# Layer 1's paired panels with feature sums as the stationary operand, and two of the last pair's four tiles scored by TensorE

## The chip, the cores and the metric

The kernel runs on one core of one Trainium2 chip. A run's time is the device time of that core in microseconds, from the start of the launch to its end. The profile is of one such execution: its span goes from the first to the last instruction, and every start time in a profile row counts from the start of that span. The engines are TensorE (PE for matrix products, PEld for loading their stationary operand), VectorE (DVE), ScalarE (ACT), GpSimd (POOL, which also issues the gathers and scatters) and SyncE (SP, which issues most transfers).

## The reference

Two layers of the same form work on 3327 tokens of 256 features, padded here to 3328 = 26 tiles of 128. Each layer first mixes tokens with the sparse matrix `adj` and then sends every token to two of eight experts.

```
x = x + relu(adj @ (ln(x) @ W) + b)                       # layer 0, mixing
x = x + sum over the 2 best of 8 experts (relu MLP, 1024 hidden) of ln(x)
A = tanh(adj*adj) where adj > 0, at most 700 entries a row # layer 1, mixing
x = x + relu(A @ (tanh(ln(x) @ Wp + bp) @ Wg) + bg)
x = x + ln(x) + sum over the 2 best of 8 experts (gelu MLP, 256 hidden) of ln(x)
```

`ln` is a layer norm without gain or offset. The two best experts come from a product with a 256 x 8 matrix, the router (plus a bias in layer 0). All arithmetic that matters here is float32.

## The kernel before

**Panels and pieces.** The output tokens of a mixing step are cut into 13 panels of 256 tokens. The transposed matrix of a panel comes in two pieces, each of 13 chunks of 128 source tokens by 256 output tokens (1664 KB). Six buffers called `ring` hold pieces; a piece that is used up gives its buffer to the next load. Layer 1 turns each piece into tanh(max(a, 0)^2) in place, by passes on DVE (line 653, where the maximum is taken) and ACT (line 660).

**Pairs by seven products.** Panels are handled two at a time where possible: layer 0 takes panels 0 and 1 singly, then (2,3) to (10,11) as pairs, then 12 singly; layer 1 takes 0 singly, (1,2) to (9,10) as pairs, then 11 and 12 singly. A pair's 2 x 2 block product (two panels, two halves of the feature columns) is done with seven block products instead of eight, from sums of pieces (`add_pieces`, line 459, in place) and sums of feature halves (`half_sums`, made once a layer and held in `pad`). Each block product is 13 chunks deep. The features themselves lie in `s`, tokens on partitions.

**Two orientations.** In layer 0 `product` (line 449) makes the feature half the stationary operand and streams 256 piece columns, so the result has features on partitions; it is copied to SBUF and multiplied by the weight matrix later (`weigh`, line 485), which brings tokens back onto partitions. In layer 1 `multiply` (line 679) makes a 128 x 128 block of the piece the stationary operand and streams 128 feature columns, twice for each chunk, so the result already has tokens on partitions. In the profile a float32 matmul has two records, so a block product is 26 records of 256 columns in layer 0 and 52 records of 128 columns in layer 1.

**What follows a pair in layer 1.** ACT copies partial results from PSUM to `h2T` tiles (line 664), DVE adds others (lines 716, 735, 740), then `add_sums` adds the bias (line 691) and takes max(., 0) plus `x` (line 692). The panels' routing (`route1`) is a dictionary of small steps that the next unit calls by name through `step`, from hooks placed between its own matmuls: statistics (DVE), normalized tiles `xn` (ACT, line 361), turned tiles `pt` (TensorE, line 388), scores `pg` by TensorE (line 826) or by DVE (line 818), the choice of two (`rt_both`, line 854), the positions `pr` (TensorE, lines 923 and 924) and at last the scatter of tokens into the experts' lists (POOL, line 945). In `single`, the hooks are counted in matmuls from 0 to 51.

**The join of layer 0's mixing and its experts.** While panel 12 of layer 0 is multiplied (line 474), `finish` weighs the panels (10, 11) and calls `route0` for their four tiles: layer norm, then eight DVE instructions for each tile (line 818) that multiply and sum `xn` with one row of the router, then the choice. The positions (line 923) of these tiles stand in TensorE's order after the first expert block's 32 hidden-layer records (line 1378) and the weighing of panel 12 (line 485).

**Order.** Each engine runs its instructions in the order in which a scheduler put them; the scheduler orders by estimated cost and data dependence, and `behind(...)` pins an instruction after another. An engine whose next instruction waits holds up everything behind it on that engine. The experts' blocks of layer 1 begin to load while panels 11 and 12 are still being multiplied; `place_of` (line 1397) is DVE's conversion of the loaded token numbers of a block into scatter indices.

Of the kernel before, what the change touches and what calls it, by code (L numbers as in the profile page):

```python
# [128 lines left out]
def gnn_moe_two_layers(  # L129
# [198 lines left out]
    last_normalized, last_shift, last_turned, last_pass = [], [], [], []  # L328
# [72 lines left out]
    def add_relu(x_tile, ps, b_sb):  # L401

        t = work.tile([P, D], F32, name="gnn_t", bufs=2)
        nc.vector.tensor_tensor(t, ps, b_sb, ALU.add)
        nc.vector.scalar_tensor_tensor(x_tile, t, 0.0, x_tile, ALU.max, ALU.add)
# [55 lines left out]
    def aggregate_first(b_sb, w, w_sb, begin, count, route, listed, freed):  # L461
# [29 lines left out]
        def finish():  # L491
            if not waiting:
                return
            todo = list(waiting)
            waiting.clear()
            if todo[0][0] < NPAN - 1:
                listed()
            for pan, g in todo:
                for it in range(PW // P):
                    weigh(pan, g, it)  # L500
            if todo[0][0] == NPAN - 1:
                listed()
            for _ in route([pan for pan, _ in todo]):
                pass
# [123 lines left out]
        rest(NPAN - 1, 0, {CJ: layer0.turn_first}, LAST_BEHIND)  # L628
        return finish

    def aggregate(b_sb, route, freed, turn, copied):
# [31 lines left out]
        def copy(out, ps):  # L663
            copied.append(nc.scalar.copy(out, by_tile(ps)))

        def sums_of():

            g = work.tile([P, 2, D], F32, name="h2T", bufs=2)
            return g, [g[:, :, ts(h, P)] for h in range(DC)]

        def by_tile(ps):
            return ps.rearrange("p (i d) -> p i d", d=P)

        def multiply(ps, a, b, first=True, hooks=()):
            hooks = dict(hooks)
            ps = by_tile(ps)
            for c in range(CJ):
                for it in range(PW // P):
                    nc.tensor.matmul(  # L679
                        ps[:, it, :], lhsT=a[:, c, ts(it, P)], rhs=b[:, c, :],  # L680
                        start=(first and c == 0 and it == 0), stop=(c == CJ - 1),
                        skip_group_check=True,
                    )
                if c in hooks:
                    hooks[c]()

        b_tiles = b_sb.unsqueeze(1).to_broadcast([P, 2, D])

        def add_sums(pan, g):
            x_t = x[:, pan * 2 : pan * 2 + 2, :]  # L690
            nc.vector.tensor_tensor(g, g, b_tiles, ALU.add)
            nc.vector.scalar_tensor_tensor(x_t, g, 0.0, x_t, ALU.max, ALU.add)

        def pair(p1, p2, step, ps_x, ps_q, ps_b, ps_z):
# [4 lines left out]
            multiply(ps_x, a11, b11)  # L699
            (g1, (c11, c12)), (g2, (c21, c22)) = sums_of(), sums_of()  # L700
            copy(c11, ps_x)
# [6 lines left out]
            multiply(ps_q, a22, t4)  # L708
            copy(c21, ps_q)
# [5 lines left out]
            multiply(ps_b, a12, b21)  # L715
            nc.vector.tensor_tensor(c11, c11, by_tile(ps_b), ALU.add)
# [3 lines left out]
            multiply(ps_z, a21, t1, hooks={2: turn_, 7: turn_})  # L720
            run(1)
            copy(c22, ps_z)
            free(p2, 0)
            score = lambda: step("scores")
            multiply(ps_x, a22, t2, False, {2: score, 6: score})
            step("weights")
            copy(c12, ps_x)
# [5 lines left out]
            multiply(ps_z, a12, b22, False)  # L733
            free(p1, 1)
            nc.vector.tensor_tensor(c12, c12, by_tile(ps_z), ALU.add)
            add_sums(p1, g1)
            multiply(ps_x, a11, t3, False, {2: lambda: step("listed"), 8: lambda: step("planned")})
            filter_next(True)
            for part in (c21, c22):
                nc.vector.scalar_tensor_tensor(  # L740
                    part, part, -1.0, by_tile(ps_x), ALU.mult, ALU.subtract
                )
            add_sums(p2, g2)
# [37 lines left out]
        for u in UNITS[1]:  # L781
# [3 lines left out]
            else:  # L785
                hooks = {
                    0: lambda: step("statistics", "normalized"),
                    2: lambda: step("other scores"),
                    16: lambda: step("turned"),
                    18: lambda: step("turned"),  # L790
                    28: lambda: step("scores"),
                    30: lambda: step("scores", "weights", "exponentials"),
                    42: lambda: step("listed"),
                    48: lambda: step("planned"),
# [14 lines left out]
    def scores(xns, n, all_n=None):  # L809
        sc = work.tile([P, all_n or n, E], F32, name="rt_sc", bufs=2)  # L810
        for g in range(n):
            score_tile(xns[g // 2][:, g % 2, 0, 0:D], sc[:, g, :])
        return sc
# [401 lines left out]
    def experts(xlist, ys, group, fixed, n_hidden, func, w1T, b1, w2T, b2, copy, order_of_places, kept=None,  # L1215
# [176 lines left out]
        def place_of(t, late):  # L1392
            xb, col, n = loaded[t][1], col_of(t), groups_of(t)
            index = work.tile([P, SG], I32, name="index", bufs=6)[:, 0:n]
            with behind(last_y):
# [235 lines left out]
    f1_r_sb = const.tile([P, DC, E], F32, name="f1_r_sb")  # L1631
    f1_b1_sb = const.tile(list(f1_b1.shape), F32, name="f1_b1_sb")
    g1_bp_sb = const.tile(list(g1_bp.shape), F32, name="g1_bp_sb")
    for t, w in [
        (gnn_b_sb, g0_b[0:1, :].partition_broadcast(P)),
        (g1_wg_sb, g1_wg.rearrange("(c p) n -> p c n", p=P)),
        (f1_r_sb, f1_rT.rearrange("(c p) n -> p c n", p=P)),
        (f1_b1_sb, f1_b1),
# [21 lines left out]
    def route0(pans):  # L1660
# [5 lines left out]
        sc = scores(xns, n)  # L1666
# [30 lines left out]
    by_feature(None, g1_wp, proj_sb)  # L1697
    nc.gpsimd.dma_start(out=gnn_b_sb, in_=g1_bg[0:1, :].partition_broadcast(P))
# [491 lines left out]
```

## Time and profile before

| | us |
|---|---|
| median of three runs (1183.0, 1186.75, 1187.92) | 1186.75 |
| the profiled execution, whole time | 1181.27 |
| its span | 1179.5 |
| TensorE busy (97% of the span) | 1138.9 |
| VectorE busy (72%) | 851.9 |
| ScalarE busy (51%) | 603.9 |
| GpSimd busy (27%) | 318.5 |

The mean granted TensorE clock over the span is 0.991 of full speed. The span falls into layer 0's mixing (to about 309 us), its experts (to about 692 us), the features of layer 1 (to about 744 us), layer 1's panel 0 (to 767 us), its five pairs (767 to 981 us), panels 11 and 12 (981 to 1037 us), its experts (to about 1161 us) and the last outputs. A matmul's duration in a row is longer than its distance to the next one, since matmuls overlap; costs on TensorE are therefore read from the distance between the starts of neighbouring groups in the timeline, not from durations. A row of the timeline gives start, length, engine, line, operation, result and inputs, shape, count, and in brackets the idle time before it and what ended that idle time.

### The profile page before, as it was taken

How to read it: one execution, taken by the hardware profiler on the slowest of the kernel's cores; microseconds unless marked ns; L12 is line 12 of the kernel's file. 1: busy time of each engine (PE TensorE's matmuls, PEld its weight loads, DVE VectorE, ACT ScalarE, POOL GpSimd, SP SyncE). 2: the span in 40 equal slices, each digit the busy share in tenths (PEclk: the TensorE clock that was granted, in tenths of full speed). 3: DMA queues.
4: the chain of work that ended last, by engine and by line, in shares of the span. 5: the costliest groups of instructions: out<-in, count | busy, mean ns of one | idle time of the engine just before them, and what ended most of it. 6: DMA issues, size and time to landing. Idle time of an engine off the chain costs nothing. (4 is left out here: it accounts for less than half of the span.)

```text
span 1179.5 us, 21265 instructions
## 1 busy us (share of the span) xinstructions
PE 1138.9 (97%) x7093; PEld 1018.9 (86%) x7093; DVE 851.9 (72%) x2667; ACT 603.9 (51%) x1110; POOL 318.5 (27%) x367
## 2 busy tenths in 40 slices
PE   8999999999899999999999999999999997999983
PEld 7888888888788888888898888899999997888862
DVE  6799999988975555454545669486898896886464
ACT  5599657450323333434333336988769774043331
POOL 2211232242331112111111010022245244365442
PEclk9999999999999999999999999999999998999997
DMA  9895737724376555857665956125536633377696
GB/s 348 187 316 217 258 118 234 259 91 151 130 258 231 193 188 185 276 183 242 209 206 182 376 209 229 61 104 206 186 141 211 218 136 130 96 250 236 222 298 229
DMA packets 123190, 241.78 MB, mean 205 GB/s; under 512 B 24480, under 2 KB 93120, under 8 KB 116160
## 3 DMA queue, kind: packets, MB, share of 16 engines
q1 hardware_dynamic: 108656, 205.59, 52.3%
q0 software_dynamic: 11136, 31.60, 7.2%
q10 hardware_dynamic: 3280, 3.15, 0.8%
q8 instruction: 58, 0.95, 0.3%
q14 instruction: 60, 0.49, 0.1%
HBM read 203.98 MB, written 36.33 MB: 204 GB/s over the span
## 5 line engine op out<-in xcount | busy, mean ns | idle before, releaser
L1386 ACT ACTIVATE pad<-ps_h,ring 128x256 f32<-128x256 f32 (+1 forms) x282 | 128.6, 457 | 281.4 <-PE ps_h L1378 153.5
L1378 PE MATMUL ps_h<-pad,ring 128*128 128x256 f32 (+1 forms) x1184 | 253.4, 366 | 3.5 <-ACT pad L1328 3.2
L1378 PEld LDWEIGHTS ps_h<-pad,ring 128*128 128x128 f32 x1184 | 200.2, 190 | 46.1 <-ACT pad L1386 10.0
L945 POOL DMA_INDIRECT ys<-pad,index x114 | 115.8, 1016 | 360.3 <-DVE pad L1433 236.0
L459 DVE TENSOR_TENSOR ring<-ring,ring 128x768 f32<-128x768 f32 (+1 forms) x160 | 169.5, 1102 | 0.0
L660 ACT ACTIVATE ring<-ring 128x3328 f32<-128x3328 f32 x54 | 160.1, 2978 | 0.9 <-DMA ring<-in_adjT 0.6
L945 POOL DMA_INDIRECT xlist<-xn,rt_idx x104 | 121.2, 1165 | 126.4 <-DVE rt_idx L934 51.2
L1647 ACT ACTIVATE sign<-ring,below 128x416 bf16<-128x416 f32 x208 | 133.4, 641 | 12.5 <-DMA ring<-in_adjT 6.6
L818 DVE SCALAR_TENSOR_TENSOR rt_product<-xn,gate 128x256 f32<-128x256 f32 x272 | 122.7, 451 | 15.1 <-ACT xn L361 5.5
L679 PE MATMUL ps_g<-pad,ring 128*128 128x128 f32 x1040 | 123.5, 276 | 0.0
L679 PEld LDWEIGHTS ps_g<-pad,ring 128*128 128x128 f32 x1040 | 119.2, 192 | 0.0
L449 PE MATMUL ps_g<-ring,pad 128*128 128x256 f32 x520 | 115.0, 380 | 0.0
L449 PEld LDWEIGHTS ps_g<-ring,pad 128*128 128x128 f32 x520 | 98.5, 190 | 13.2
L1433 DVE SCALAR_TENSOR_TENSOR pad<-ps_y,ring,pad 128x128 f32<-128x128 f32 x176 | 59.3, 348 | 47.5 <-PE ps_y L1426 47.3
L449 PE MATMUL ps_g<-ring,s 128*128 128x256 f32 x390 | 89.6, 379 | 0.0
L679 PE MATMUL ps_g<-s,ring 128*128 128x128 f32 x780 | 89.5, 275 | 0.0
L679 PEld LDWEIGHTS ps_g<-s,ring 128*128 128x128 f32 x780 | 88.4, 192 | 0.1
L449 PEld LDWEIGHTS ps_g<-ring,s 128*128 128x128 f32 x390 | 74.1, 190 | 10.1
L474 PE MATMUL ps_g<-ring,s 128*128 128x256 f32 x312 | 69.2, 381 | 4.4 <-ACT s L361 4.2
L474 PEld LDWEIGHTS ps_g<-ring,s 128*128 128x128 f32 x312 | 58.8, 190 | 13.8 <-ACT s L361 5.2
L753 PE MATMUL ps_g<-s,ring 128*128 128x256 f32 x312 | 70.1, 384 | 0.0
L753 PEld LDWEIGHTS ps_g<-s,ring 128*128 128x128 f32 x312 | 59.6, 193 | 8.0
(251 smaller groups left out, 1676.2 us busy)
## 6 DMA issues: line engine op xcount, KB each, us to landing
ring<-in_adjT SPq DMA_DIRECT2D x50, 1664.0 KB, 8.1
ring<-in_f_w1T SPq DMA_DIRECT2D x30, 1024.0 KB, 6.2
ring<-in_f_w2T SPq DMA_DIRECT2D x30, 1024.0 KB, 8.5
ring<-xlist SPq DMA_DIRECT2D x52, 258.0 KB, 3.5
ring<-in_f_w SPq DMA_DIRECT2D x36, 256.0 KB, 4.0
ring<-ys SPq DMA_DIRECT2D x12, 512.0 KB, 5.1
ring<-in_f_b SPq DMA_DIRECT2D x34, 128.0 KB, 7.7
xlist<-h2T SPq DMA_DIRECT2D x16, 257.0 KB, 5.9
```

Source lines behind the costliest of these rows:

```text
L449: nc.tensor.matmul(ps, lhsT=b[:, c, :], rhs=a[:, c, :], start=(first and c == 0), stop=(c == CJ - 1), skip_group_check=not first,)
L459: nc.vector.tensor_tensor(out[:, part, :], out[:, part, :], other[:, part, :], ALU.add)
L474: nc.tensor.matmul(sums[pan][c], lhsT=s[:, j, ts(c, P)], rhs=piece(pan, j // CJ)[:, j % CJ, :], start=(j == 0), stop=(j == NT - 1),)
L660: last_pass[:] = [nc.scalar.activation(a, a, f)]
L679: nc.tensor.matmul(ps[:, it, :], lhsT=a[:, c, ts(it, P)], rhs=b[:, c, :], start=(first and c == 0 and it == 0), stop=(c == CJ - 1), skip_g ...
L753: nc.tensor.matmul(banks_[it], lhsT=piece(pan, k)[:, c, ts(it, P)], rhs=s[:, j, :], start=(j == 0), stop=(j == NT - 1),)
L818: nc.vector.scalar_tensor_tensor(product, xn, 1.0, gate[:, e, :], ALU.mult, ALU.mult, accum_out=sc[:, e : e + 1],)
L945: d = nc.gpsimd.indirect_dma_start(out=a[:, :], out_offset=bass.IndirectOffsetOnAxis(ap=index, axis=0), in_=rows_, in_offset=None,)
L1378: last_product[:] = [nc.tensor.matmul(ps, lhsT=w1[:, c, ts(hc, P)], rhs=xT[:, c, :], start=(c == 0), stop=(c == DC - 1),)]
L1386: nc.scalar.activation(hT[:, hc, :], ps, func, bias=bb1[:, hc : hc + 1])
L1433: last_y[:] = [nc.vector.scalar_tensor_tensor(part, ps, xb[:, g, WT : WT + 1], part, ALU.mult, ALU.add)]
L1647: nc.scalar.activation(sign, piece(pan, k)[:, :, ts(i, GROUP)], AF.Sign, bias=below, accum_out=positive[:, pan, i, k : k + 1],)
```

## The change

Layer 1's pairs use layer 0's orientation: `product` with the feature half or feature sum stationary and 256 piece columns streamed. The result has features on partitions, so ACT's copies add the bias per partition (`b_plus`, or `b_minus` where the sign is turned later), and the separate bias addition on DVE goes. A finished panel is put in the list `outputs_`; `add_output`, called from a hook inside a later product, turns it with four 128 x 128 TensorE transposes into a PSUM tile and lets DVE add max(., 0) to `x`. For the second panel of a pair this hook lies in the next unit's first product, after its fifth chunk; for the first panel in the pair's own last product, after its sixth. The routing hooks of `single` move to later chunks. The conversion `place_of` of layer 1's first block is pinned after the last panel's addition to `x` instead of after the last expert output. In layer 0, the last pair's first two tiles are turned and scored by TensorE (16 of the 32 scoring instructions of DVE go), in three steps of `route0` that run as hooks of panel 12. Two small tables and one copy of layer 0's router are loaded on POOL's queue.

```
-        def copy(out, ps):
-            copied.append(nc.scalar.copy(out, by_tile(ps)))
...
-        def multiply(ps, a, b, first=True, hooks=()):
...
-        def add_sums(pan, g):
-            x_t = x[:, pan * 2 : pan * 2 + 2, :]
-            nc.vector.tensor_tensor(g, g, b_tiles, ALU.add)
-            nc.vector.scalar_tensor_tensor(x_t, g, 0.0, x_t, ALU.max, ALU.add)
+        def copy(out, ps, bias):
+            copied.append(nc.scalar.activation(out, ps, AF.Identity, bias=bias))
+
+        outputs_ = []
+
+        def add_output():
+
+            if not outputs_:
+                return
+            pan, g = outputs_.pop(0)
+            pt = psh.tile([P, 2, D], F32, name="ps_o", tag="ph")
+            for it in range(2):
+                for h in range(DC):
+                    nc.tensor.transpose(pt[:, it, ts(h, P)], g[:, h, ts(it, P)], ident)
             x_t = x[:, pan * 2 : pan * 2 + 2, :]
+            nc.vector.scalar_tensor_tensor(x_t, pt, 0.0, x_t, ALU.max, ALU.add)
...
-            multiply(ps_x, a11, b11)
-            (g1, (c11, c12)), (g2, (c21, c22)) = sums_of(), sums_of()
-            copy(c11, ps_x)
+            product(ps_x, b11, a11, hooks={4: add_output})
+            g1, g2 = (work.tile([P, DC, PW], F32, name="h2T", bufs=2) for _ in range(2))
+            copy(g1[:, 0, :], ps_x, b_plus[:, 0:1])
             step("statistics")
...
-            nc.vector.tensor_tensor(c12, c12, by_tile(ps_z), ALU.add)
-            add_sums(p1, g1)
-            multiply(ps_x, a11, t3, False, {2: lambda: step("listed"), 8: lambda: step("planned")})
+            nc.vector.tensor_tensor(g1[:, 1, :], g1[:, 1, :], ps_z, ALU.add)
+            outputs_.append((p1, g1))
+            product(
+                ps_x, t3, a11, False,
+                {2: lambda: step("listed"), 5: add_output, 8: lambda: step("planned")},
+            )
             filter_next(True)
-            for part in (c21, c22):
-                nc.vector.scalar_tensor_tensor(
-                    part, part, -1.0, by_tile(ps_x), ALU.mult, ALU.subtract
-                )
-            add_sums(p2, g2)
+            nc.vector.scalar_tensor_tensor(
+                g2, g2, -1.0, ps_x.unsqueeze(1).to_broadcast([P, DC, PW]), ALU.mult, ALU.subtract
+            )
+            outputs_.append((p2, g2))
             free(p1, 0)
...
-                    0: lambda: step("statistics", "normalized"),
-                    2: lambda: step("other scores"),
-                    16: lambda: step("turned"),
-                    18: lambda: step("turned"),
-                    28: lambda: step("scores"),
-                    30: lambda: step("scores", "weights", "exponentials"),
-                    42: lambda: step("listed"),
-                    48: lambda: step("planned"),
+                    4: add_output,
+                    6: lambda: step("statistics", "normalized", "other scores"),
+                    27: lambda: step("turned"),
+                    34: lambda: step("scores", "weights", "exponentials"),
+                    48: lambda: step("listed"),
+                    50: lambda: step("planned"),
...
-            with behind(last_y):
+            with behind(last_relu if kept and t == 0 else last_y):
                 if t < EARLY:
                     nc.vector.tensor_copy(index, xb[:, :, ID])
...
-        rest(NPAN - 1, 0, {CJ: layer0.turn_first}, LAST_BEHIND)
+        hooks = {CJ: layer0.turn_first, CJ + 7: turn_last_pair, NT - 1: score_last_pair}
+        rest(NPAN - 1, 0, hooks, LAST_BEHIND)
...
         xns = normalized(t, n, on_scalar=n == 4)
         yield
-        sc = scores(xns, n)
+        if pans[-1] == NPAN - 2:
+            xnT = by_features(xns[0], 2, "h2T")
+            yield
+            sc = scores([None] + xns[1:], n, range(2, n))
+            scores_by_product(xnT, 2, f0_wg_sb, sc[:, 0:2, :])
+        else:
+            sc = scores(xns, n)
         yield
...
+    with nc.allow_non_contiguous_dma("a few hundred elements"):
+        nc.gpsimd.dma_start(out=b_plus, in_=g1_bg[0, :].rearrange("(c p) -> p c", p=P))
+    nc.gpsimd.tensor_scalar(b_minus, b_plus, -1.0, None, ALU.mult)
```

## The prediction

> **What bounds the kernel now.** I read the page first, then the list of waits on TensorE, then TensorE's timeline, and DVE's only where TensorE stood still.
>
> ```profile
> span 1179.5 us, 21265 instructions
> PE 1138.9 (97%) x7093; PEld 1018.9 (86%) x7093; DVE 851.9 (72%) x2667; ACT 603.9 (51%) x1110; POOL 318.5 (27%) x367
> ```
>
> TensorE is busy for 97% of the span. The granted clock is 0.991 of full over the span. A microsecond counts if it is taken from TensorE's own work or from a gap in it. The waits on TensorE (engine, line, what it waited for, then total, times, longest in us) name the gaps:
>
> ```profile
> PE pt L388 <- ACT xn L361: 6.1, 1, 6.1
> PE ps_g L474 <- ACT s L361: 4.2, 2, 2.3
> PE pr L923 <- DVE rt_both L854: 3.8, 2, 3.1
> ```
>
> The first and the longest part of the third lie where the diff works. The 4.2 us are in the start of layer 0. Inside the five pairs there is no gap: they are TensorE work end to end, so there the cost of each product decides. TensorE's timeline for a layer 0 product, for layer 1 products, and for turning and scoring inside one:
>
> ```profile
> 64.90 5.78 PE L449 MATMUL ps_g<-ring,pad 128*128 128x256 f32 x26
> 70.52 5.78 PE L449 MATMUL ps_g<-ring,s 128*128 128x256 f32 x26
> 76.13 11.39 PE L449 MATMUL ps_g<-ring,pad 128*128 128x256 f32 x52
> ...
> 767.47 5.97 PE L679 MATMUL ps_g<-s,ring 128*128 128x128 f32 x52
> 773.27 5.97 PE L679 MATMUL ps_g<-pad,ring 128*128 128x128 f32 x52
> 779.08 5.97 PE L679 MATMUL ps_g<-s,ring 128*128 128x128 f32 x52
> ...
> 786.23 0.60 PE L388 MATMUL pt<-ident,xn 128*128 128x128 f32 x4
> 786.66 5.97 PE L679 MATMUL ps_g<-pad,ring 128*128 128x128 f32 x52
> 792.47 0.96 PE L826 MATMUL pg<-f_r_sb,xnT 128*128 128x8 f32 x8
> 793.28 4.71 PE L679 MATMUL ps_g<-pad,ring 128*128 128x128 f32 x40
> ```
>
> Take the distances between starts: two products of 26 records of 256 columns take 11.23 us (216.0 ns a record), two of 52 records of 128 columns 11.61 us (111.6 ns a record), four transposes 0.43 us, the scores of two tiles 0.81 us. And DVE where TensorE waits 6.14 us in panel 11:
>
> ```profile
> 988.87 0.16 DVE L348 SCALAR_TENSOR_TENSOR ln_nw<-ln_guess 128x4 f32<-128x4 f32 x1
> 995.89 0.17 DVE L1397 CAST index<-ring 128x2 int32<-128x2 f32 x1 [6.86 <-DMA ring<-xlist]
> ```
>
> DVE is in the middle of the layer norm of panels 9 and 10 (`ln_nw`, continued at 995.96). The next instruction in its queue is the index conversion of layer 1's first expert block (`place_of`), whose data is still being transferred. The norm, ACT's `xn` and TensorE's `pt` all wait for a number that the scatter needs only after panel 12.
>
> **The change part by part.** The sum is made against the profiled execution (1181.3 us, of which 1179.5 are span; the 1.8 outside stay). It is 5.5 us below the median of the runs, 1186.75, so I carry the difference over to the median.
>
> *Products.* Five pairs of seven products change from 52 records of 128 columns to layer 0's 26 of 256: 35 x (11.61 - 11.23) / 2 = 6.7 us less, all on TensorE's path. A rule speaks for a smaller gain: the Trainium skill, "TensorE: Matmul & The Clock Gate", section "Wait — 56ns, not 53.3ns?", gives each matmul a fixed 2.5 ns. 26 records fewer in 35 products would then be 2.3 us by an estimate from that figure. The rows show 7.3 ns for each record saved (2 x 111.6 - 216.0), and the new form is the very one that layer 0 runs. I take 6.7.
>
> *Transposes.* Ten panels are turned by four transposes each: 10 x 0.435 (0.43 to 0.44 between the starts of such rows) = 4.4 us more on TensorE, from the `pt` row, which stands in the middle of a product as the new ones will. Here a rule speaks against the change: the same page, "Part 4: PE-mode transpose", measured about 275 ns for one 128 x 128 transpose in a kernel and says that transposes don't keep the clock up. Forty of them would cost 11.0 us (an estimate), 6.6 more, and the total below would be a gain of 3.0 instead of 9.6. The rows show 109 ns each between matmuls, and the page's row of granted clocks stays at 9 tenths or more through the pairs, which hold such transposes already. I take 4.4 and keep 11.0 as the far end.
>
> *The first block's index.* In the built order of the changed kernel, the conversion stands behind panel 12's last addition to `x`, near 1038, by when the block landed long ago (995.9). What is late next? Times from the start of panel 11 (T = 981.4 before): DVE reads the pair's last product by about T + 1.4 after the planning instructions ahead of it, TensorE turns it after five chunks at T + 2.2, then DVE has some 3 us of planning, the addition to `x` (0.7) and the norm (3.7): the shift is ready near T + 9, the first two `xn` near T + 10. The transposes `pt` stand after 28 matmuls and the four extra transposes, 28 x 0.432 + 0.4 = T + 12.5. So 2 us are to spare, and the 6.14 us go whole. The positions `pr` come at T + 22.8; DVE needed 14.4 us from the shift to `rt_both` before (996.5 to 1010.9), so T + 23.4: a wait of 0.6, as the 0.67 before. Gain 6.1.
>
> *Layer 0's last pair.* TensorE idles 3.09 us for `rt_both`:
>
> ```profile
> 309.20 0.17 PE L923 MATMUL pr<-rt_both,before 128*128 128x8 bf16 x1 [3.09 <-DVE rt_both L854]
> ```
>
> 32 scorings of DVE (290.5 to 306.3, 0.47 us each with their read-out) stand ahead of it. Sixteen go: DVE ends them near 299, the choice takes 3 more, 302; `pr` stands near 307. The wait goes whole. TensorE pays a transposition (0.43) and a scoring (0.81). Are these ready? ACT's first `xn` are done near 291; the transposes come after 18 of 26 chunks, near 293. Gain 3.09 - 1.24 = 1.8.
>
> *At no cost on the path.* DVE loses the bias additions (10 x 0.69), and its two 0.4 us subtractions become one of 0.7: idle time there. ACT's twenty copies with bias take about 0.47 (the row of line 1386) instead of 0.37; ACT waits up to 5.9 us for TensorE in each pair and covers it; without that cover it would be 2 us. POOL gets two small loads and one instruction: `b_plus` and `b_minus` are queued before the `gate` load, which waits until 39.4 anyway; the router copy takes 0.74 where POOL is idle until 58.5. `b_plus` is 256 single elements among the first loads. The nearest row, 2048 such elements, landed in 24.2 us, so an eighth is 3.0 us, spread beside other transfers: between 0 and 1 us on a start that waits for data. Moving `proj_sb` and the bias behind POOL's copies at 312 delays nothing before 692.
>
> *New waits.* In-order TensorE now waits for DVE at each of ten turnings. DVE at the end of a pair:
>
> ```profile
> 846.66 0.42 DVE L735 TENSOR_TENSOR h2T<-h2T,ps_g 128x256 f32<-128x256 f32 x1 [1.85 <-PE ps_g L679]
> ...
> 847.73 1.89 DVE L653 TENSOR_SCALAR ring<-ring 128x3328 f32<-128x3328 f32 x1
> ...
> 852.75 0.75 DVE L740 SCALAR_TENSOR_TENSOR h2T<-h2T,ps_g 128x256 f32<-128x256 f32 x2 [1.23 <-PE ps_g L679]
> ```
>
> Second panels: DVE starts 0.2 us after the product and needs 0.75 (line 740, both parts); TensorE comes after 2.16 us. First panels: the last sum is done 0.6 us after its product; TensorE comes after 2.8. The additions to `x` of second panels end about 1.0 us later than before in the pair, so the sums of pieces do too: the fourth product had 2.2 us to spare (its sum ends at 824.8, it starts at 827.05) and keeps about 1. Each turning also needs a semaphore record of 51 ns on TensorE, if nothing hides it. I put 0.3 for these and 0.3 for the start; the bounds are 0 and 7 (ten times 0.7).
>
> Sum: -6.7 + 4.4 - 6.1 - 1.8 + 0.6 = -9.6, so 1171.7 for the profiled execution, **1177.1** for the median.
>
> **The rivals.**
> *The change is mostly eaten* (no change to measure). Either transposes cost the page's price (-9.6 + 6.6 = -3.0, 1183.7), or each turning waits some 0.7 us (-9.6 + 6.4 = -3.2, 1183.5). Against both stand the `pt` rows and the idle time that DVE shows just before lines 735 and 740 (1.2 to 1.9 us); for them, that every new transpose sits on the one engine without slack.
> *DVE's queue becomes the bound* (slower). Between the two results of a pair DVE has the 1.9 us maximum pass over a new piece (line 653), and it waits for that piece's transfer. If the transfer is late, the second panel's result is late, and now TensorE stands behind it, in each of five pairs; before, only `x` did. The slack is about 1.2 us; to end 5.9 us slower than before, a pair must lose 3.1 us, so the piece must be over 4 us late each time: 1171.7 + 15.5 = 1187.2 profiled, 1192.7. The trace has one such wait in twelve, of 0.2 us.
> *The index wait returns.* Should the norm's chain be slow for another reason, up to 3 us of the 6.1 stay: -6.6, 1180.2. This is still faster.
>
> **How the numbers follow.** The three runs differ by 0.4%, so 0.5%, 5.9 us, is about what a measurement can tell from no change. My forecast has a chance of 0.70, the index rival 0.10 (both faster: 0.80), the eaten gain 0.14, the slower case 0.06. Low end: all small costs zero, the start unharmed and a run as low as the fastest of the three against its median (-3.75): 1172.8, and 3 more for second-order gains on DVE, 1170. High end 1186: the eaten gain with a run above its median by 1.2 and another 1.1 of waits.
>
> **What would show it.** Right: line 449 with 26-record groups 5.61 apart in layer 1; ten groups of four transposes of 0.43; a pair 42.9 (809.63 to 852.55) - 7 x 0.19 + 2 x 0.43 = 42.4 us long; no wait of `pt` for `xn` above 1 us; none of `pr` at 309; `index` without a long wait. Wrong: waits of the new transposes for `h2T` on DVE, of line 449 for sums of pieces, or a later first matmul.

## The result, and the profile after

| | before | after |
|---|---|---|
| first comparison, median us | 1184.88 (4 runs, 1182.47 to 1187.92) | 1171.04 (4 runs, 1169.6 to 1174.0) |
| ratio, 95% interval | | 0.9885 (0.9851 to 0.9919) |
| second comparison, median us | 1185.83 (9 runs, 1183.49 to 1188.76) | 1171.25 (5 runs, 1170.61 to 1171.53) |
| ratio, 95% interval | | 0.9878 (0.9859 to 0.9896) |
| the profiled execution of the first comparison, us | 1181.27 | 1174.0 |

The kernel is faster by 13.8 to 14.6 us (differences of the medians). The forecast was 1177.1, from -9.6 us. The two profiled executions of the first comparison lie only 7.3 us apart: the one of before, 1181.27, lies below all four of its timed runs, the one of after is the slowest of its four. So a reading of these two alone shows half of the gain. I therefore read stages, and read them in the profiles of all kernels below.

The page of the changed kernel, its head:

```profile
span 1172.3 us, 19508 instructions
PE 1138.2 (97%) x6235; PEld 994.7 (85%) x6235; DVE 837.8 (71%) x2621; ACT 606.6 (52%) x1111; POOL 315.8 (27%) x370
```

TensorE is as busy as before (1138.9), in 858 fewer records. The waits on TensorE (total us, times, longest us):

```profile
PE ptb L1325 <- ACT pad L1387: 3.9, 3, 2.3
PE ps_g L474 <- ACT s L361: 3.0, 2, 1.6
PE ps_h L1379 <- ACT pad L1329: 2.8, 3, 1.7
PE ps_y L1427 <- DVE xnT L1418: 1.5, 1, 1.5
PE ps_g L449 <- DMA ring<-in_adjT: 1.4, 1, 1.4
```

The 6.1 us of `pt` for `xn` and the 3.8 us of `pr` for `rt_both` are gone. Three rows have grown: `ptb` (1.6 before), `xnT` (0.4 before), and the transfer `in_adjT`, which had none. TensorE's timeline at a pair's last products and at the turning of its second panel in the next pair:

```profile
815.03 5.78 PE L449 MATMUL ps_g<-ring,pad 128*128 128x256 f32 x26
820.64 5.78 PE L449 MATMUL ps_g<-ring,s 128*128 128x256 f32 x26
...
851.43 2.32 PE L449 MATMUL ps_g<-ring,s 128*128 128x256 f32 x10
853.59 0.60 PE L691 MATMUL ps_o<-ident,h2T 128*128 128x128 f32 x4
854.02 3.62 PE L449 MATMUL ps_g<-ring,s 128*128 128x256 f32 x16
```

A product takes 5.61 us, four transposes take 0.43, and no row has a wait in brackets. DVE at this turning:

```profile
851.63 0.69 DVE L743 SCALAR_TENSOR_TENSOR h2T<-h2T,ps_g 128x512 f32<-128x512 f32 x1 [1.06 <-PE ps_g L449]
...
854.22 0.69 DVE L693 SCALAR_TENSOR_TENSOR x<-ps_o,x 128x512 f32<-128x512 f32 x1 [1.91 <-PE ps_o L691]
```

The result is there at 852.32, TensorE comes for it at 853.59: 1.27 us of slack. Panel 11 on TensorE, and the moved index conversion on DVE:

```profile
978.89 2.32 PE L756 MATMUL ps_g<-s,ring 128*128 128x256 f32 x10
981.04 0.60 PE L691 MATMUL ps_o<-ident,h2T 128*128 128x128 f32 x4
981.48 10.09 PE L756 MATMUL ps_g<-s,ring 128*128 128x256 f32 x46
991.41 0.60 PE L388 MATMUL pt<-ident,xn 128*128 128x128 f32 x4
...
1001.81 0.17 PE L924 MATMUL pr<-rt_both,before 128*128 128x8 bf16 x1
...
1027.55 0.44 DVE L405 SCALAR_TENSOR_TENSOR x<-gnn_t,x 128x256 f32<-128x256 f32 x1
1027.92 0.16 DVE L1398 CAST index<-ring 128x2 int32<-128x2 f32 x1
```

Neither the transposes (12.5 us after the panel's start) nor the positions (22.9 us after it) wait, and the conversion waits for nothing. The end of layer 0's mixing:

```profile
294.24 0.60 PE L388 MATMUL pt<-ident,xn 128*128 128x128 f32 x4
...
299.00 0.95 PE L827 MATMUL pg<-f_wg_sb,h2T 128*128 128x8 f32 x8
...
308.53 0.17 PE L924 MATMUL pr<-rt_both,before 128*128 128x8 bf16 x1
```

The new transposes and scores stand inside panel 12, and the positions come without a wait.

**The stages of all profiles.** Every column is a distance in us on TensorE's timeline. "First pair": from the span's start to the first product with an operand in `pad`. "Mixing 0": from there to the first block's turning (`ptb`) in panel 12 of layer 0. "Join": on to the second block's hidden layer. "Experts 0": on to the transposes of layer 1's features. "Pairs": from the first pair of layer 1 to panel 11. "Panel 11": on to the first block's turning in panel 12, 150 product records. "Last": from layer 1's first hidden layer to TensorE's last matmul. The stages left out (features and panel 0, 74.8; the rest of panel 12, 13.1) are equal in all; what follows TensorE's last matmul, 16.7 to 20.2 us, is not in the table and scatters too.

| kernel | first pair | mixing 0 | join | experts 0 | pairs | panel 11 | last |
|---|---|---|---|---|---|---|---|
| before | 64.90 | 221.61 | 30.48 | 375.65 | 213.97 | 42.97 | 123.30 |
| after | 66.05 | 221.71 | 28.35 | 376.79 | 211.15 | 34.86 | 126.31 |
| after again (e5) | 64.77 | 221.63 | 28.35 | 376.69 | 211.14 | 35.09 | 124.04 |
| index only (e1) | 67.92 | 224.75 | 32.06 | 375.97 | 213.97 | 38.05 | 126.15 |
| layer 0 only (e2) | 65.09 | 221.71 | 28.35 | 378.36 | 213.97 | 43.90 | 125.06 |
| pairs and hooks only (e3) | 63.98 | 221.61 | 32.04 | 380.19 | 211.15 | 44.43 | 126.33 |
| turned four times (e4) | 65.40 | 221.71 | 28.35 | 376.63 | 223.06 | 35.74 | 127.26 |
| wait filled (e7) | 65.45 | 221.71 | 32.04 | 375.78 | 213.98 | 44.31 | 127.39 |
| second result late (e8) | 64.61 | 221.64 | 28.36 | 377.02 | 214.96 | 37.16 | 124.43 |
| index, wait filled (e9) | 64.78 | 224.49 | 31.88 | 375.74 | 213.97 | 37.74 | 123.43 |
| old hooks (e10) | 65.11 | 221.72 | 28.35 | 376.91 | 211.14 | 37.00 | 123.49 |
| stores later (e6) | 64.83 | 221.61 | 28.35 | 376.82 | 211.14 | 34.94 | 122.68 |
| stores two later (e11) | 64.98 | 221.61 | 28.35 | 376.81 | 211.14 | 34.78 | 122.07 |

What the change sets repeats to 0.02 us (pairs, and the join with its edit). What transfers set, the first pair and the last stage, moves by 1 to 5 us from execution to execution, with the same code. The 66.05 and the 126.31 of the first profile of after belong to that. So do the 3 us more of mixing 0 in e1 and e9: with the same instructions as before up to there, DVE waits 10.6 and 12.5 us for the load of a bias (`gnn_b_sb`), and the first pairs wait after it. Whether other runs of e1 have this is not recorded.

### The profile page after: what moved, and what is told of

Its sections match the earlier page's. It is cut to its first block, busy times and chain, and to the rows that moved or that the text cites. A ratio compares the mean times of both kernels' runs of the same rounds, so it can differ in the third digit from the quotient of the medians.

```text
span 1172.3 us, 19508 instructions
## 1 busy us (share of the span) xinstructions
PE 1138.2 (97%) x6235; PEld 994.7 (85%) x6235; DVE 837.8 (71%) x2621; ACT 606.6 (52%) x1111; POOL 315.8 (27%) x370
## 5 line engine op out<-in xcount | busy, mean ns | idle before, releaser
L449 PE MATMUL ps_g<-ring,pad 128*128 128x256 f32 x1040 | 235.6, 381 | 1.4 <-DMA ring<-in_adjT 1.4
L449 PEld LDWEIGHTS ps_g<-ring,pad 128*128 128x128 f32 x1040 | 194.9, 190 | 27.0 <-DMA ring<-in_adjT 1.8
L449 PE MATMUL ps_g<-ring,s 128*128 128x256 f32 x780 | 176.8, 379 | 0.0
L449 PEld LDWEIGHTS ps_g<-ring,s 128*128 128x128 f32 x780 | 147.9, 190 | 19.9
L819 DVE SCALAR_TENSOR_TENSOR rt_product<-xn,gate 128x256 f32<-128x256 f32 x256 | 116.6, 456 | 15.0 <-ACT xn L361 6.2
L474 PE MATMUL ps_g<-ring,s 128*128 128x256 f32 x312 | 69.0, 380 | 3.0 <-ACT s L361 3.0
L474 PEld LDWEIGHTS ps_g<-ring,s 128*128 128x128 f32 x312 | 58.8, 190 | 11.9 <-ACT s L361 3.9
L756 PEld LDWEIGHTS ps_g<-s,ring 128*128 128x128 f32 x312 | 58.8, 190 | 7.9
L1418 DVE TENSOR_TENSOR xnT<-pad 128x512 f32<-128x512 f32 x22 | 15.2, 692 | 59.5 <-ACT pad L1387 59.5
L1476 PE MATMUL ps_y<-ring,pad 128*128 128x256 f32 x224 | 52.4, 379 | 0.0
L1476 PE MATMUL ps_y<-s,pad 128*128 128x256 f32 (+1 forms) x200 | 49.7, 388 | 0.1
L929 POOL COPY xn<-rt_w 128x4 f32<-128x4 f32 x26 | 4.5, 199 | 162.7 <-DVE rt_w L892 162.7
```

The costliest lines, as they stand in the source:

```text
L449: nc.tensor.matmul(ps, lhsT=b[:, c, :], rhs=a[:, c, :], start=(first and c == 0), stop=(c == CJ - 1), skip_group_check=not first,)
L474: nc.tensor.matmul(sums[pan][c], lhsT=s[:, j, ts(c, P)], rhs=piece(pan, j // CJ)[:, j % CJ, :], start=(j == 0), stop=(j == NT - 1),)
L756: nc.tensor.matmul(banks_[it], lhsT=piece(pan, k)[:, c, ts(it, P)], rhs=s[:, j, :], start=(j == 0), stop=(j == NT - 1),)
L819: nc.vector.scalar_tensor_tensor(product, xn, 1.0, gate[:, e, :], ALU.mult, ALU.mult, accum_out=sc[:, e : e + 1],)
L1476: last_product[:] = [nc.tensor.matmul(ps, lhsT=hT[:, hc, ts(g, P)], rhs=w2[:, hc, :], start=(hc == 0), stop=(hc == hc_n - 1),)]
```

## The experiments

**e1: the index alone.**

```
+        last_relu[:] = [nc.vector.scalar_tensor_tensor(x_tile, t, 0.0, x_tile, ALU.max, ALU.add)]
...
-            with behind(last_y):
+            with behind(last_relu if kept and t == 0 else last_y):
```

> The kernel before, with one edit: the index conversion of layer 1's first expert block is pinned behind panel 12's addition to x. As predicted: the 6.14 us wait of the transposes in panel 11 goes and nothing else, -6.1 us in the time. Theory W, formed from the two traces (the transposes and the 14 product records just after that wait ran 0.53 and 1.1 us slower than the same ones of the changed kernel, with a granted clock of 0.68 around them): a long wait also costs about 1.6 us of slower matmuls after it, so -7.8 us. Rival: the norm's chain is slow for another reason and some 3 us of wait stay, -3. In the profile: 104 records of panel 11, from its first matmul to the next panel's, 1.6 us more or less apart tells the first two apart.

Measured: ratio 0.9958 (0.9941 to 0.9976), 1182.53 us against 1188.38 of before beside it. Panel 11 is 4.9 us shorter (38.05 for 42.97): less than the prediction and theory W said, more than the rival. (The interval of the times, -2.9 to -7.0 us, holds the -6.1 and, just, the -3, and rules out W's -7.8. The profiled execution is the slowest of e1's twelve.) The first wait is gone, the second has grown from 0.67 to 2.02, and the matmuls behind it are slow. The timeline, and then the windows (after each window: its length, then busy time and instructions of PE, PEld, DVE, ACT and POOL, then the granted clock, DMA share and GB/s):

```profile
1012.48 0.18 PE L923 MATMUL pr<-rt_both,before 128*128 128x8 bf16 x1 [2.02 <-DVE rt_both L854]
```

```profile
1010.00:1013.00 3.00, 0.97 (x9) 0.54 (x8) 3.00 (x15) 0.00 (x0) 0.00 (x0) 0.96 0.61 163
1013.00:1016.00 3.00, 3.00 (x10) 2.28 (x10) 1.31 (x11) 0.21 (x1) 0.33 (x3) 0.50 0.87 265
1016.00:1019.00 3.00, 3.00 (x15) 2.58 (x15) 1.08 (x3) 0.00 (x0) 2.39 (x3) 0.97 0.26 89
```

For three microseconds after the wait the granted clock is 0.50: ten records run where fifteen do at full clock. So in this execution the index alone is worth 4.9 us; where the clock is kept it would be some 6.6, an estimate: the 60 product records behind the wait take 15.1 us here and 13.4 in before. What is late next is the positions, not the transposes.

**e2: layer 0's last pair alone.**

```
+        hooks = {CJ: layer0.turn_first, CJ + 7: turn_last_pair, NT - 1: score_last_pair}
+        rest(NPAN - 1, 0, hooks, LAST_BEHIND)
...
+            sc = scores([None] + xns[1:], n, range(2, n))
+            scores_by_product(xnT, 2, f0_wg_sb, sc[:, 0:2, :])
```

> The kernel before, with one edit: the first two tiles of layer 0's last pair are turned and scored by TensorE. As predicted: the 3.09 us wait for the positions goes, 1.24 us are paid, -1.8 us. Rival: the gain is given back before layer 0's experts end, because DVE there waits for a weight transfer (in the changed kernel's trace the lead of 0.8 us before 674 is gone at 692): 0. In the profile the second block's hidden layer (316.99 before) should start 1.8 to 2.1 us earlier relative to panel 12's start, and the features of layer 1 (692.64) earlier by as much or not at all.

Measured: ratio 0.9981 (0.9970 to 0.9991), 2.7 us between the medians. The join takes 28.35, as in every kernel with this edit. Without the edit it takes 30.48 in one profile and 31.88 to 32.06 in four: the wait is 3.05 to 3.09 us in all five, and in four of them slow matmuls follow. In e3:

```profile
308.23 0.17 PE L924 MATMUL pr<-rt_both,before 128*128 128x8 bf16 x1 [3.05 <-DVE rt_both L855]
...
308.80 2.77 PE L1476 MATMUL ps_y<-ring,pad 128*128 128x256 f32 x6
```

Six records fill 2.56 us there (308.80 to 311.36) instead of 1.30. So the join gains 2.1 or 3.6. The rival is right in part. In the eight profiles with the edit, experts 0 takes 376.63 to 378.36; in four of the five without it, 375.65 to 375.97. DVE in the changed kernel shows what holds:

```profile
665.98 0.69 DVE L1346 TENSOR_TENSOR gate<-ring 128x512 f32<-128x512 f32 x1 [1.39 <-DMA ring<-in_f_w2T]
```

The weights of a late block arrive when they do, and a TensorE that is earlier waits for DVE 1.3 to 1.7 us near 676 instead of 0.4. About 1 us of the lead goes there. (e3, without the edit, has a wait of 2.96 at the same place; why is open.) Join and experts 0 together have a median of 407.8 without the edit and 405.2 with it: -2.6, which is what the times show.

**e3: pairs and hooks alone.**

```
-            with behind(last_relu if kept and t == 0 else last_y):
+            with behind(last_y):
...
-        hooks = {CJ: layer0.turn_first, CJ + 7: turn_last_pair, NT - 1: score_last_pair}
+        hooks = {CJ: layer0.turn_first}
```

> The changed kernel without the edit of the index and without the edit of layer 0: pairs in the new orientation and the moved hooks of the single panels. As predicted: the pairs give -6.7 + 4.4 + 0.3 = -2.0 us from the start of the first pair to the start of panel 11 (-2.8 in the changed kernel's trace). Rival, by the price of 275 ns for a transpose: +4.3 us. The wait in panel 11 was predicted as a matter of the index alone (6.1 stays), in all -2. Theory H (hooks): the hook of the transposes stands 11 chunk matmuls later, so the same late index makes TensorE wait only about 3 us instead of 6.1, and the slow matmuls after it are fewer: in all about -6 us.

Measured: ratio 1.0002 (0.9988 to 1.0017), -1.4 to +2.1 us: nothing. The pairs gain their 2.82 us to the hundredth, so the orientation does what it should, and the rival price of transposes is out. But theory H fell. DVE and TensorE in panel 11:

```profile
998.09 0.17 DVE L1398 CAST index<-ring 128x2 int32<-128x2 f32 x1 [7.95 <-DMA ring<-xlist]
```

```profile
1000.63 0.93 PE L388 MATMUL pt<-ident,xn 128*128 128x128 f32 x4 [4.14 <-ACT xn L361]
...
1014.23 0.18 PE L924 MATMUL pr<-rt_both,before 128*128 128x8 bf16 x1 [1.02 <-DVE rt_both L855]
```

With the index still late, the moved hooks shorten the first wait only to 4.14, and the clock falls after it and after the second one: panel 11 takes 44.43, 1.5 more than before. (Pairs and panel 11 together then give -1.4, at the edge of the interval; where the rest goes is open.) In these profiles the index without the hooks gives -4.9, the hooks without the index +1.5; together they gain 8.1.

**e4: what a transpose costs.**

```
-            for it in range(2):
-                for h in range(DC):
-                    nc.tensor.transpose(pt[:, it, ts(h, P)], g[:, h, ts(it, P)], ident)
+            for _ in range(4):
+                for it in range(2):
+                    for h in range(DC):
+                        nc.tensor.transpose(pt[:, it, ts(h, P)], g[:, h, ts(it, P)], ident)
```

> The changed kernel with each of the ten turnings done four times over (120 more transposes of 128 x 128, same result). By the row of four transposes in 0.435 us: 30 x 0.435 = +13.1 us, all of it in the five pairs (10 of 11 turnings' worth before panel 11's end). By the price of 275 ns each: +33 us. If TensorE waited at the turnings for something else that these hide, less than +13: the turning would then not be what costs.

```profile
809.47 2.32 PE L449 MATMUL ps_g<-ring,s 128*128 128x256 f32 x10
811.63 1.91 PE L692 MATMUL ps_o<-ident,h2T 128*128 128x128 f32 x16
813.38 3.62 PE L449 MATMUL ps_g<-ring,s 128*128 128x256 f32 x16
```

Sixteen transposes take 1.75 us. Nine of the ten turnings lie before panel 11, and the pairs grow by 223.06 - 211.15 = 11.91 us for 27 groups more: 0.441 a group, 110 ns a transpose. The ratio is 0.9982 (0.9970 to 0.9995), 0.0104 or 12.3 us above the changed kernel's. The products alone then gained 2.82 + 9 x 0.441 = 6.79 us, if no turning waited; the rows show no such wait, and their distances say the same: 35 x (11.61 / 2 - 5.61) = 6.8.

**e5: the changed kernel again.**

> The changed kernel itself, unedited, timed beside the kernel before as often as the single edits were. The three edits alone measured ratios of 0.9958 (index), 0.9981 (layer 0) and 1.0002 (pairs and hooks): if their effects add, 0.994 (-7 us). As predicted: -9.6 us, 0.992. By the stages of the two traces, with the slower matmuls after each removed wait counted in (layer 0's join -2.1 to -3.7, pairs -2.8, panel 11 -8.1): -13 to -14.7 us, 0.988.

The ratio 0.9878 (0.9859 to 0.9896), -14.6 us, agrees with the sum of stages: pairs -2.8, panel 11 -7.9 to -8.1, join and experts 0 -2.6, in all -13.3 to -13.5. The three single edits do not add up to it (0.9958, 0.9981 and 1.0002 give 0.994): index and hooks are one change.

**e10: the changed kernel with the hooks of before.**

```
-                    27: lambda: step("turned"),
-                    34: lambda: step("scores", "weights", "exponentials"),
-                    48: lambda: step("listed"),
-                    50: lambda: step("planned"),
+                    16: lambda: step("turned"),
+                    18: lambda: step("turned"),
+                    28: lambda: step("scores"),
+                    30: lambda: step("scores", "weights", "exponentials"),
+                    42: lambda: step("listed"),
+                    48: lambda: step("planned"),
```

> The changed kernel with the single panels' later routing hooks (turned, scores, weights, listed, planned) at the chunk matmuls of before. TensorE then reaches panel 11's positions after 43 instead of 49 product matmuls, about 20.3 us after the panel's start, and DVE has them ready at 22.9. If the moved hooks are what removed this wait, TensorE waits 2.6 us, and panel 11's stage is 37.0 us (clock kept) to 38.6 us (clock lowered after the wait), against 34.9 to 35.1 of the changed kernel. As predicted, where the index alone was the gain and the hooks had no term: 35.

```profile
1000.58 0.18 PE L926 MATMUL pr<-rt_both,before 128*128 128x8 bf16 x1 [2.02 <-DVE rt_both L857]
```

Panel 11 takes 37.00, as expected for a clock that is kept: the moved hooks are worth 2.0 us of wait, and some 1.7 more where the clock falls, as in e1. (Its one run, 1172.29 us, is too little to show this in the time.) DVE has the positions' input ready 22.5 to 23.1 us after the panel's start, whichever hooks; the old ones brought TensorE there too early.

**e7 and e9: is it the idleness that slows the matmuls?** Both put bf16 matmuls that nobody reads ahead of a wait in panel 11, e7 into the kernel before, e9 into e1.

```
+        def fill():
+            ps = psh.tile([P, P], F32, name="ps_fill", tag="ph")
+            with tc.issue_after(last_mm[0].ins):
+                for _ in range(36):
+                    nc.tensor.matmul(ps, lhsT=ones_sq, rhs=ones_sq, start=True, stop=True)
...
+                if u[0] == NPAN - 2:
+                    hooks[39] = fill
```

(e7: 80 of them, at hook 15.)

> The kernel before, with the index where it was; 80 bf16 matmuls that nobody reads stand in TensorE's queue just ahead of the transposes that wait in panel 11, so that TensorE is busy for most of the wait. If the wait costs only its length, nothing changes: 43.0 us from panel 11's start to the turning after the first half of panel 12. If idleness lowers the clock for some 3.4 us after it, the transposes and the 14 product records behind them run at full speed (0.44 and 3.02 us apart instead of 0.97 and 4.12): 41.3 us, -1.6.

e7 missed. The 80 matmuls ran before the wait rather than in it, and five product matmuls moved behind the transposes:

```profile
990.71 4.63 PE L752 MATMUL ps_fill<-ones_sq 128*128 128x128 bf16 x80
...
999.44 0.97 PE L388 MATMUL pt<-ident,xn 128*128 128x128 f32 x4 [3.62 <-ACT xn L361]
```

3.62 us of idleness stayed, and the slow transposes with it (one run, 1187.08 us). It tells nothing between the theories. (It could not have gained 1.6 in any case: in before, DVE has the positions' input ready only 29.5 us after the panel's start, so a quicker TensorE would have waited there.)

> The kernel with the index edit alone (e1), and 36 bf16 matmuls that nobody reads (2.0 us) in TensorE's queue during panel 11, 11 product matmuls after its scores: they fill the 2.02 us for which TensorE waited there for the positions. In e1 the 15 product matmuls that followed the wait were 1.6 us slow (clock 0.50 for some 3 us). If it is idleness that lowers the clock, the clock stays at 1.00 and the stage from panel 11's start to the next expert turning is 37.2 us (22.95 until the positions, 32 matmuls of 0.432 and the positions' own 0.4); if the wait costs its length and the slow matmuls have another cause, 38.8.

```profile
1004.31 2.17 PE L752 MATMUL ps_fill<-ones_sq 128*128 128x128 bf16 x36
...
1008.82 0.18 PE L933 MATMUL pr<-rt_both,before 128*128 128x8 bf16 x1 [0.98 <-DVE rt_both L864]
...
1009.55 14.06 PE L761 MATMUL ps_g<-s,ring 128*128 128x256 f32 x64
```

```profile
1009.00:1012.00 3.00, 2.87 (x18) 2.44 (x16) 1.90 (x13) 0.20 (x1) 0.35 (x2) 1.00 0.87 254
```

The clock stays at 1.00, the 64 records behind the wait run 217 ns apart, and the stage takes 37.74 (one run, 1180.43 us), with a wait of 0.98 where the expectation had it filled. This agrees with idleness as the cause. It is no proof by itself, since e10 kept its clock with the same 2.02 us unfilled. By their length alone, waits look like a chance: after those of 3.6 us and more in panel 11 the clock fell each time (before, e2, e3, e7), after the one of 3.05 to 3.09 at the join in four of five, after the one of 2.02 in panel 11 in one of two. A fall cost 1.4 to 2.3 us in these places, and 3.1 in e1's first pair, where it lasted 6.8 us.

The granted clock itself says more. In all 13 traces it changes only on a grid of 3.41 us steps; a fall lasts one step or two, and the grid lies differently in each execution. The two waits of 2.02 cut at these steps, first e1, then e10:

```profile
1009.35:1012.76 3.41, 1.39 (x12) 0.87 (x10) 3.38 (x16) 0.00 (x0) 0.00 (x0) 1.00 0.70 204
1012.76:1016.17 3.41, 3.41 (x13) 2.60 (x13) 1.55 (x13) 0.21 (x1) 0.50 (x3) 0.50 0.82 247
```

```profile
996.26:999.67 3.41, 2.30 (x11) 1.69 (x9) 3.20 (x13) 0.00 (x0) 0.00 (x0) 1.00 0.68 196
999.67:1003.08 3.41, 2.47 (x17) 2.06 (x18) 3.06 (x21) 0.20 (x1) 0.32 (x2) 1.00 0.72 231
```

In e1 the whole wait lies in one step, TensorE is busy for 1.39 us of it, and the next step is at 0.50. In e10 the wait is divided between two steps, neither busy for less than 2.30, and the clock stays. The join is alike: before kept its clock with 1.72 us busy in the emptier of its two steps, e3 lost it with 0.52 in one. Of the 4228 steps between 45 us and TensorE's last matmul, the 18 with TensorE busy for 41% or less were all followed by a step at 0.50; of the others, all 45% or more, two were (58% in e3, 81% in e1, this one itself at 0.50). So what decides is how much of a wait falls into one step. By this count e9's fill did keep the clock: without it, its step from 1004.49 to 1007.91 would have been busy for some 1.34 us, 39% (an estimate from the rows). This is read from the traces; no experiment moved the steps themselves.

**e8: the rival made true by hand.**

```
+            for _ in range(6):
+                nc.vector.tensor_tensor(g2, g2, g2, ALU.max)
             outputs_.append((p2, g2))
```

> The changed kernel, with six additional DVE instructions in each pair that rewrite the second panel's result with itself just before it may be turned (0.61 us each in the queue, 3.65 in all). It makes the rival 'DVE's queue becomes the bound' true by hand. The trace shows 1.27 us between DVE's end and the turning: by that slack each of the five second turnings then waits 2.4 us, 12 us in all, and more (up to 1.6 us each, 20 in all) where the clock falls after the wait. If the hook's place leaves more slack than that, less than 12.

```profile
851.33 0.69 DVE L743 SCALAR_TENSOR_TENSOR h2T<-h2T,ps_g 128x512 f32<-128x512 f32 x1 [0.72 <-PE ps_g L449]
852.05 4.32 DVE L747 TENSOR_TENSOR h2T<-h2T 128x512 f32<-128x512 f32 x6
```

```profile
851.13 5.34 PE L449 MATMUL ps_g<-ring,s 128*128 128x256 f32 x24
856.43 0.66 PE L691 MATMUL ps_o<-ident,h2T 128*128 128x128 f32 x4
```

A miss: the scheduler knows these instructions' cost and put the turning behind 24 records instead of 10. Only one of the five second turnings waits, 0.43 us in panel 11, where the positions then wait 1.50. The pairs cost 3.8 us more and panel 11 2.1 to 2.3; the one run took 1176.58. So DVE can be 4.3 us longer in each pair (the row's six take 4.32, not the 3.65 expected) for 0.76 us of the pair. What a late transfer would do, which the scheduler cannot know, was not tried.

**e6 and e11: the tail.** In the first profile of after the last stage lost 3 us against before. ScalarE and TensorE there:

```profile
1140.74 0.38 ACTq L1995 DMA_DIRECT2D out_x<-x  x1
1141.22 0.63 ACT L1387 ACTIVATE pad<-ps_h,ring 128x128 f32<-128x128 f32 x2 [3.13 <-DVE pad L1483]
```

```profile
1141.65 0.44 PE L1325 MATMUL ptb<-ident,ring 128*128 128x128 f32 x2 [2.26 <-ACT pad L1387]
```

ScalarE's queue has a store of tokens (`out_x`) ahead of the activations. The store waits for DVE's last addition to `x`, which ends at 1140.71 and itself waited for rows (`ring<-ys`). e6 pins each store behind the last activation of the newest block's hidden layer (`hidden_`), which is one block later; e11 lets one more block pass (`store_added(at - 3)` for `at - 2`):

```
                     t, n = added.pop(0)[0]
-                    nc.scalar.dma_start(out=rows_of(out, t, n), in_=x[:, t : t + n, :])
+                    with behind(hidden_):
+                        nc.scalar.dma_start(out=rows_of(out, t, n), in_=x[:, t : t + n, :])
```

> The changed kernel, with one edit in the last stage: each store of finished tokens on ScalarE's queue is issued one expert block later. In the trace these stores wait for DVE's additions of output rows, which wait for transfers, and hold up the hidden layer's activations behind them and so TensorE (5.7 us of waits between 1118 and 1142 and slow matmuls after the longest). If the stores are what holds TensorE up, those waits go and the stage from the first hidden layer to TensorE's last matmul shrinks from 126.3 to about 120 to 122 us: -4 to -6 us against the changed kernel. Rival: DVE's own wait for the rows delays its work on the expert outputs and TensorE waits for that instead: 0.

Measured: 1167.88 us (5 runs, 1167.38 to 1169.5) beside 1171.25 (1170.61 to 1171.53) of the changed kernel; ratio to before 0.9848 (0.9829 to 0.9866). This version beats both kernels. Of TensorE's five waits between 1118 and 1142 three are gone. The first, 1.66, stays (nearly every kernel here has it), and one of 2.10, where the last store still stands right behind its addition:

```profile
1139.49 0.40 ACTq L1998 DMA_DIRECT2D out_x<-x  x1
1140.01 0.63 ACT L1388 ACTIVATE pad<-ps_h,ring 128x128 f32<-128x128 f32 x2 [2.97 <-DVE pad L1485]
```

> The changed kernel with each store of finished tokens two expert blocks later instead of one (e6). One store still stood right behind its addition in e6 (its wait held ScalarE 2.5 us and TensorE 2.1 us). If the stores are what holds TensorE up, that wait goes too: the last expert stage 122.7 to about 120 us, 1166 us. Rival, DVE's own wait for rows: no change against e6, 1168.

e11 gave no more: 1169.24 us (4 runs), ratio 0.9868 (0.9851 to 0.9885), its interval overlapping e6's. Its last stage is 122.07, and TensorE still waits 1.60 us for ScalarE at 1137.53, because DVE waits for rows by then:

```profile
1134.16 0.69 DVE L1574 TENSOR_TENSOR x<-x,ring 128x512 f32<-128x512 f32 x1 [3.19 <-DMA ring<-ys]
```

So the stores were the nearer cause, and the rows' transfers are the next. How much of the 3.4 us between the medians lies where is open: the last stages of the profiles of e5, its fastest run, and e6, its slowest, differ by 1.4.

## Why the prediction was right, and where its terms were not

The sign and the mechanisms held, and the time lay inside the range, near its low end: 6 us below the number. That the range held it is in part luck: its low end came from a fast run (3.75) and 3 us of unnamed gains on DVE, and the surplus came from neither. Term by term, with the stages:

- *Products, -6.7.* Measured -6.8 (e4 with the pairs' stage, and the rows' distances). The distance between rows held; the fixed cost of 2.5 ns a matmul from the Trainium skill's page "TensorE: Matmul & The Clock Gate" would have given 2.3, an estimate.
- *Transposes, +4.4.* Measured 0.441 for four (e4), 4.4 for ten. The same page's 275 ns would have given 11.0, and 29.7 for e4's 27 groups (estimates), where 11.9 were measured. That transposes let the clock fall was not seen: the pairs' stage repeats to 0.01 us with 36 of them inside.
- *New waits, +0.3.* None in the pairs: no turning there has a wait in its row, and 6.8 from the rows' distances less 9 x 0.441 = 3.97 leaves the measured 2.82. The start's 0.3 cannot be told from its scatter of 1 us.
- *The index, -6.1.* This is the step that failed in size. With the turning that lies in it, panel 11 should have shortened by 5.7; it shortened by 8.1 (42.97 to 34.86), and e2's 43.90 would make it 9.0. The sum took waits at their length: the 6.14, and a second wait of 0.6 that would stay "as the 0.67 before" (measured: none). The trace of before held more than this. One of its windows:

```profile
990.00:1000.00 10.00, 3.86 (x15) 2.82 (x14) 2.31 (x8) 2.54 (x5) 3.63 (x7) 0.68 0.54 160
```

  After the wait the clock was lowered: the transposes took 0.97 for 0.44 and the next 14 records 4.12 for 3.02, 1.6 us that go with the wait. I had looked at the clock only as a row of tenths over the span, where this hides in one digit. And the moved hooks had no term. I counted where they put TensorE (22.8 after the panel's start; measured 22.9) but not what would have happened without them: e10 shows 2.0 us of wait, e1 that and a lowered clock.
- *Layer 0's last pair, -1.8.* Measured -2.1 in the join between the first two profiles, -3.6 against the four other profiles without the edit, where the clock fell after the same wait; 1.0 of it is given back near 676. Net -2.6. The give-back had no term: I had asked what is late next at the positions, not 370 us later.
- *From the profiled execution to the median.* I carried the 5.5 us between them over unchanged. They were not a constant: before, the clock falls or not after the join's wait, 1.6 us of them; after, that wait no longer exists. Where the rest lies is open.

The same page of the Trainium skill, section "What's actually happening", has a window of about 3.4 us that runs freely and halves the clock when it was idle. The traces' grid of 3.41 us agrees. Half speed for 3.4 us costs 1.7, an estimate from that figure, near most of the measured 1.4 to 2.3, and a free window fits that the same wait costs it or not. It would have told me to add to each wait of over 3 us something between 0 and 1.7. Its section "Why this matters for your kernels" sets the limit at gaps of about 3 us; e1 shows a fall after 2.02, with its window busy for 41%.

Of the rivals, "mostly eaten" is out by e4 and by the pairs without waits, and "the index wait returns" by the trace. "DVE's queue becomes the bound" did not come: the second result keeps its 1.27 us of slack, and e8 shows what 4.3 us more work would do.

## What to carry to other kernels

Price a wait on the engine that is never idle with what follows it: its length, and the slow matmuls after it, read from windows of a few microseconds around it; whether they come depends on where the wait falls on the clock's steps, so it is still a chance over executions. Ask what is late next with and without each hook that moves, since two edits that each fall short alone can be the whole gain together. When two profiles differ by less than the medians, compare stages across several profiles: those that repeat to hundredths are the change, those that scatter are not.

## What was not expected of the hardware

- The lowered clock after short waits: 0.50 of full for 3 us after a wait of 2.02 us in e1, 1.00 after the same wait in e10, as the steps of 3.41 us divide it; 0.71 between 1141.6 and 1145.0 in the first profile of after, behind waits of 0.62 and 2.26.
- A store issued from ScalarE's queue holds its activations for as long as its data is late: 3.1 us in the first profile of after, at the cost of 2.3 on TensorE.
- bf16 matmuls of 128 x 128 that load their stationary operand each time take 55.8 ns one after another (36 in 2.01 us, 80 in 4.46 us), half of a float32 transpose.
